# A four-layer graph network on one core: GpSimd's clear behind each gather, 400 bytes in place of 200

## The chip, the cores and the metric

The kernel runs on one core of a Trainium2 chip. The metric is the device time of one execution in microseconds (us), as the median of several executions. The profile is that of one further execution; its times are counted from the start of its span. The engines are TensorE (PE, with its weight loads as PEld), VectorE (DVE), ScalarE (ACT), GpSimd (POOL) and SyncE (SP).

## The reference

The input is x (2708 nodes, 128 features) and a square matrix adj of 2708 x 2708 with some 0.6% of its entries nonzero (and the diagonal). Four layers follow each other, each one as `x = layernorm(x + layer(x, adj))`:

```python
# layer 0: weighted mean
msg = adj.T @ x;  out = msg / adj.sum(axis=0)[:, None]
# layer 1: messages along the edges
messages = gelu((x @ Ws.T)[:, None] + (x @ Wd.T)[None] + b)     # i, j, d
agg = einsum('ijd,ij->id', messages, adj)
out = layernorm(gelu(concat([x, agg]) @ upd_w.T + upd_b) + x) * ln_w + ln_b
# layer 2: h = adj @ (x @ W) + b, batch norm over the nodes, leaky relu
# layer 3: attention, four heads, each
E = leaky_relu((x @ w1)[:, None] + (x @ w2)[None], 0.01)        # i, j, d
s = exp(8 * tanh((E @ a) / 8)) * adj;  s = s / s.sum(-1)
head = leaky_relu(s @ x @ Wlin.T, 0.01);  out = concat(heads) @ w
```

In layers 1 and 3 only the nonzero entries of adj count, so the kernel computes them for the edges alone.

## The kernel before

**Lists.** Layer 0 loads adj by blocks of 128 rows (22 blocks, the last of 20 rows), sums with TensorE, and has VectorE search each row for its nonzero entries. The rows are ranked by their number of entries and their lists scattered to DRAM in that order (lists_dram), in two groups (blocks 0 to 12 and 13 to 21 of the order). Read back, they give a list of neighbours per row (`idx`, `idx3`).

**Layer 1, 22 turns.** A turn handles one block of 128 ranked rows with up to CAPS[b] neighbours each (22 for block 1, 12 for block 11; blocks 0 and 13 have 30 and 29). The turns go in the order TURNS (0 to 18, 21, 19, 20). `messages` takes the neighbours in chunks of up to 8: for each neighbour number k, one gather on GpSimd's queue brings 128 rows of 512 bytes from d_dram, chosen by a column of `idx`, into a slice of a tile `msg` (5 buffers of 8 slices). Then VectorE adds the row's own term to the whole chunk (L907), ScalarE takes the gelu, and VectorE weighs and sums the slices (L895). `update` finishes the block on PE, ACT and DVE and scatters the rows (x_n) to x2_dram from GpSimd's queue (L266). In the first turns the search of the remaining rows and the scatters of their lists run beside this, and the transposing of adj to at_dram; from turn 11 on blocks of layer 2 run (`layer2`, whose gather of at_rows is on GpSimd's queue too). Turn 13 is the first that needs the lists of the second group.

**Layer 2's end.** Batch norm and layer norm over all nodes; t2_dram gets a row per node: 512 transformed features, 128 features, 4 scores (2576 bytes). x3_dram gets the nodes in ranked order by 22 scatters.

**Layer 3, 100 quads.** A quad is four gathers into one tile `g` (9 buffers, GOT), each of 120 to 128 rows of t2_dram chosen by a column of `idx3`. For each quad PE repeats the own terms (z), VectorE adds them (L1566), then multiplies (L1392, L1384), ScalarE sums (L1400), and the softmax and the weighted sum follow two quads at a time. Each of the 24 groups of rows (BLOCKS3) ends in a scatter to the output (out_dram, L266) on GpSimd's queue. PE, DVE and ACT have an order written by hand here (`manual_schedule`); GpSimd's queue does not.

**Order on GpSimd.** The framework's planner orders GpSimd's instructions and assigns buffers, with extra edges where the kernel states them. `gather_spaced` (L258) is used for the gathers of layers 1 and 3: it puts a clear of a small tile `pause` behind each gather and holds the next gather from the same table behind that clear:

```python
    def gather_spaced(dst, table, index):
        before = paused.get(table.name)
        with tc.issue_after(before) if before is not None else nullcontext():
            did = gather(dst, table, index)
        with tc.issue_after(did.ins):
            paused[table.name] = nc.gpsimd.memset(pause, 0).ins
```

Nothing reads `pause`. The gathers of at_rows and all scatters are issued without such a clear.

Of the kernel before, what the change touches and what calls it, by code (L numbers as in the profile page):

```python
# [28 lines left out]
I8 = mybir.dt.int8  # L29
# [56 lines left out]
def gnn_resnorm_kernel(  # L86
# [120 lines left out]
    keep = ctx.enter_context(tc.tile_pool(name="keep", bufs=1))  # L207
# [31 lines left out]
    ones = keep.tile([P, P], FP, name="ones")  # L239
    nc.gpsimd.memset(ones, 1.0)  # L240

    pause = keep.tile([1, 200], I8, name="pause")

    def natural(dram, b0, b1):

# [1862 lines left out]
```

## Time and profile before

| what | value |
|---|---|
| median of 10 runs | 1643.79 us (1632.72 to 1648.18) |
| the profiled execution | 1643.97 us, span 1642.3 us |
| mean granted TensorE clock | 0.709 |
| busy: PE, DVE, ACT, POOL | 1166.6, 1168.7, 772.2, 1094.4 us |
| gathers and clears in layer 1 | 368 each, the gathers starting from 201.0 to 827.7 us |
| gathers and clears in layer 3 | 400 each, the gathers starting from 938.2 to 1577.2 us |

How to read it: a line of costliest groups gives line, engine, operation, output<-input and count, then busy us, mean ns of one, and the idle time of the engine before these instructions with what ended it ("issue": the engine waited for nothing that the profile shows). A line of the timeline gives start, duration, engine, line, operation, and in brackets the idle time before it with its releaser. A gather's span on GpSimd is that of its instruction there, not of the transfer. In the lines of windows, each engine has its busy us and number of instructions.

### The profile page before, as it was taken

What the parts mean: (1) busy time and instruction counts of PE and PEld (TensorE: products, weight loads), DVE (VectorE), ACT (ScalarE), POOL (GpSimd) and SP (SyncE); (2) the same over time, 40 slices, a digit from 0 to 9 for tenths busy, and PEclk for the clock granted to TensorE, in tenths of its full rate; (3) what the DMA queues carried; (4) which work ended last, traced back from release to release, by engine and by line L of the source; (5) the groups of instructions that cost most, each with busy time, mean ns of one, the idle gap of its engine ahead of it and who ended that gap; (6) DMA issues with size and microseconds to landing.
All of it is one profiled execution on the core that took longest, in us unless ns stands there. A gap on an engine that the chain in (4) does not pass through costs nothing. (4 is left out here: it accounts for less than half of the span.)

```text
span 1642.3 us, 24406 instructions
## 1 busy us (share of the span) xinstructions
PE 1166.6 (71%) x5771; PEld 817.5 (50%) x5771; DVE 1168.7 (71%) x4895; ACT 772.2 (47%) x3156; POOL 1094.4 (67%) x1771
## 2 busy tenths in 40 slices
PE   6995523356366664476774787988899988988994
PEld 6984412245245453466663344544455545545553
DVE  8999657387665563556538486888888787788882
ACT  3447566365344321112213455566565566565662
POOL 1002588887787668887722588887887777878730
PEclk9997655555555586687866867677876777777675
DMA  8842476588566724444422677877786765867630
GB/s 260 320 144 94 128 180 178 171 232 243 145 155 177 209 95 114 168 134 170 142 83 76 212 240 198 232 229 206 208 246 187 202 194 164 229 175 228 185 94 8
DMA packets 167682, 289.68 MB, mean 176 GB/s; under 512 B 49600, under 2 KB 121502, under 8 KB 160429
## 3 DMA queue, kind: packets, MB, share of 16 engines
q0 software_dynamic: 60496, 190.77, 40.3%
q1 hardware_dynamic: 99489, 92.57, 18.5%
q10 hardware_dynamic: 7544, 4.69, 1.2%
q8 instruction: 48, 0.79, 0.2%
q14 instruction: 105, 0.86, 0.2%
HBM read 242.51 MB, written 45.36 MB: 175 GB/s over the span
## 5 line engine op out<-in xcount | busy, mean ns | idle before, releaser
L249 POOL DMA_INDIRECT g<-t_dram,idx x400 | 403.7, 1009 | 100.5 <-issue 67.4
L249 POOL DMA_INDIRECT msg<-d_dram,idx x368 | 350.7, 953 | 87.8 <-issue 69.8
L1400 ACT ACTIVATE sum_junk<-g 126x128 bf16<-126x128 f32 (+3 forms) x1024 | 300.7, 295 | 112.9 <-DVE g L1392 76.2
L1369 PE MATMUL z<-x,copies 32*126 32x512 f32 (+3 forms) x800 | 209.0, 880 | 26.4 <-DVE g L1566 25.6
L980 PE MATMUL pt_a<-ident,rows 128*128 128x128 f32 (+2 forms) x475 | 114.0, 394 | 137.4 <-ACT at_sb L985 136.7
L263 POOL MEMSET pause<- 1x200 int8 x768 | 195.5, 255 | 0.1
L1400 ACT ACTIVATION_READ_ACCUMULATOR sum_junk<-g 126x1 f32 (+3 forms) x1024 | 191.5, 187 | 0.0
L1029 PE MATMUL acc<-x_nat,at_rows 128*128 128x128 f32 (+2 forms) x968 | 148.5, 316 | 54.8 <-DMA at_rows<-at_dram,perm 54.5
L1566 DVE TENSOR_TENSOR g<-g,z 126x1536 f32<-126x1536 f32 (+3 forms) x100 | 174.8, 1748 | 12.4 <-PE z L1369 12.4
L1374 PE MATMUL z<-g,ident 126*126 126x512 f32 (+3 forms) x200 | 162.7, 907 | 13.0 <-DMA g<-t_dram,idx 13.0
L1029 PEld LDWEIGHTS acc<-x_nat,at_rows 128*128 128x128 f32 (+2 forms) x968 | 135.4, 223 | 65.3 <-DMA at_rows<-at_dram,perm 52.2
L980 PEld LDWEIGHTS pt_a<-ident,rows 128*128 128x128 f32 (+2 forms) x475 | 82.0, 203 | 162.2 <-ACT at_sb L985 159.4
L1392 DVE SCALAR_TENSOR_TENSOR g<-g,a_ps 126x1536 f32<-126x1536 f32 (+6 forms) x100 | 151.1, 1511 | 0.0
L431 PE MATMUL acc<-x_nat,rows 128*128 128x129 f32 (+3 forms) x1012 | 127.6, 287 | 26.5 <-DMA rows<-in_adj_dram 15.6
L895 DVE SCALAR_TENSOR_TENSOR own<-msg,ls,own 128x128 f32<-128x128 f32 (+1 forms) x302 | 105.6, 350 | 53.6 <-ACT msg L910 49.7
L431 PEld LDWEIGHTS acc<-x_nat,rows 128*128 128x128 f32 (+2 forms) x1012 | 121.9, 196 | 31.8 <-DMA rows<-in_adj_dram 16.7
L1446 PE MATMUL po_s<-wm,g 126*128 126x24 f32 (+6 forms) x800 | 114.9, 296 | 31.3 <-DVE wm L1433 29.6
L1446 PEld LDWEIGHTS po_s<-wm,g 126*128 126x128 f32 (+3 forms) x800 | 111.2, 220 | 46.7 <-DVE wm L1433 40.5
L985 ACT COPY at_sb<-pt_a 128x512 f32<-128x512 f32 (+3 forms) x154 | 68.3, 475 | 85.5 <-DMA at_dram<-at_sb 84.1
L1374 PEld LDWEIGHTS z<-g,ident 126*126 126x126 f32 (+3 forms) x200 | 40.1, 251 | 129.2 <-issue 87.7
L1384 DVE SCALAR_TENSOR_TENSOR g<-z,a 126x128 f32<-126x128 f32 (+3 forms) x400 | 91.9, 285 | 13.4 <-PE z L1374 13.4
L456 DVE FIND_INDEX8 ci<-cv,rows 128x8 uint32<-128x247 f32 (+2 forms) x242 | 98.7, 408 | 0.0
(303 smaller groups left out, 2137.0 us busy)
## 6 DMA issues: line engine op xcount, KB each, us to landing
rows<-in_adj_dram SPq DMA_DIRECT2D x34, 1354.0 KB
at_dram<-at_sb SPq DMA_DIRECT2D x105, 256.0 KB
g<-t_dram,idx POOLq DMA_INDIRECT x400
msg<-d_dram,idx POOLq DMA_INDIRECT x368
t_dram<-t_row SPq DMA_DIRECT2D x21, 256.0 KB
x_s<-dx_dram SPq DMA_DIRECT2D x21, 128.0 KB
at_dram<-at_sb SPq DMA_DIRECT2D x21, 64.0 KB
t_dram<-x_nat SPq DMA_DIRECT2D x5, 256.0 KB
```

What stands on the lines that cost most here:

```text
L249: return nc.gpsimd.indirect_dma_start(out=dst, out_offset=None, in_=table[0:N, :], in_offset=bass.IndirectOffsetOnAxis(ap=index, axis=0),)
L263: paused[table.name] = nc.gpsimd.memset(pause, 0).ins
L431: nc.tensor.matmul(accs0[k][0:m, c0 : c0 + f1 - f0], lhsT=rows[0:n, j0 : j0 + m], rhs=x_nat[0:n, b, f0:f1], start=k not in started, stop=( ...
L895: nc.vector.scalar_tensor_tensor(to, m, v, last, ALU.mult, ALU.add)
L980: nc.tensor.transpose(pt[0:m, j, 0:n], rows[0:n, c0 : c0 + m], ident[0:n, 0:n])
L1029: nc.tensor.matmul(accs2[ib // 4][0:m, (ib % 4) * D : (ib % 4 + 1) * D], lhsT=at[0:n, i0 : i0 + m], rhs=xw[0:n, b, :], start=(k == 0 and i ...
L1369: nc.tensor.matmul(z3[0:e, r, :] if r < 3 else z1[0:e], lhsT=copies[g][rows, j, :], rhs=own[b][1][rows, :], start=True, stop=r < 3, skip_g ...
L1374: nc.tensor.matmul(z1[0:e], lhsT=ident[0:e, 0:e], rhs=g4[0:e, 3, 0:HD], start=False, stop=True, skip_group_check=True,)
L1392: nc.vector.scalar_tensor_tensor(z, z, 0.0, a_ps[0:e].unsqueeze(1).to_broadcast((e, count, HD)), ALU.max, ALU.mult)
L1400: nc.scalar.activation(junk[0:e], g4[0:e, r, hd * D : (hd + 1) * D], AF.Identity, accum_out=sc[0:e, r, hd : hd + 1],)
L1446: nc.tensor.matmul(po[:, p0 * HEADS : (p0 + g) * HEADS], lhsT=g4s[i][0:e, r, HD : HD + D], rhs=wm[0:e, 4 * i + r, :, :], start=True, stop= ...
L1566: nc.vector.tensor_tensor(z, z, z3[0:e], ALU.add)
```

## The change

The tile that is cleared behind each gather has 400 elements of one byte, on one partition, in place of 200. The clears stay as many, at the same places, and still nothing reads them.

```diff
-    pause = keep.tile([1, 200], I8, name="pause")
+    pause = keep.tile([1, 400], I8, name="pause")
```

## The prediction

> **What bounds the kernel now.** I first read the page's costliest groups for the two operations that the change touches, then its slices, then GpSimd's groups with shapes kept apart.
>
> ```profile
> L249 POOL DMA_INDIRECT g<-t_dram,idx x400 | 403.7, 1009 | 100.5 <-issue 67.4
> L249 POOL DMA_INDIRECT msg<-d_dram,idx x368 | 350.7, 953 | 87.8 <-issue 69.8
> L263 POOL MEMSET pause<- 1x200 int8 x768 | 195.5, 255 | 0.1
> ```
>
> There are 768 gathers (400 in layer 3, 368 in layer 1), each followed by a clear of 255 ns, and what idles before the gathers is mostly "issue", which is no waiting for anyone. The timeline of GpSimd shows one such round, and beside it what it looks like without a clear (the scatters of the late rows):
>
> ```profile
> 1200.05 0.95 POOL L249 DMA_INDIRECT g<-t_dram,idx  x1 [0.16 <-issue]
> 1201.00 0.26 POOL L263 MEMSET pause<- 1x200 int8 x1
> 1201.41 0.95 POOL L249 DMA_INDIRECT g<-t_dram,idx  x1 [0.16 <-issue]
> ...
> 297.43 0.96 POOL L266 DMA_INDIRECT dx_dram<-late,rank  x1 [0.30 <-issue]
> 298.69 0.96 POOL L266 DMA_INDIRECT dx_dram<-late,rank  x1 [0.30 <-issue]
> ```
>
> A round is 0.95 + 0.25 + 0.16 = 1.36 us; without a clear 1.26. So 0.16 (gather) and 0.30 (scatter) us of idle time are a floor, and only what is above is a wait. Then I asked for the busy time in windows cut at the stages (columns: PE, PEld, DVE, ACT, POOL, granted clock, DMA share, GB/s):
>
> ```profile
> 201.00:250.00 49.00, 13.68 (x62) 9.40 (x60) 26.97 (x114) 27.92 (x44) 43.27 (x72) 0.58 0.74 190
> 250.00:588.00 338.00, 178.75 (x768) 142.04 (x769) 217.84 (x1105) 155.81 (x321) 255.71 (x404) 0.57 0.68 188
> 588.00:766.00 178.00, 107.00 (x707) 94.84 (x705) 91.75 (x352) 36.86 (x97) 153.06 (x245) 0.73 0.41 128
> 766.00:868.00 102.00, 74.97 (x458) 64.80 (x456) 50.53 (x211) 19.39 (x56) 52.09 (x84) 0.77 0.35 119
> 990.00:1578.00 588.00, 524.98 (x2212) 297.28 (x2206) 478.20 (x1652) 346.93 (x2094) 478.59 (x745) 0.74 0.73 206
> ```
>
> From 201 to 250 and from 588 to 766 POOL is busy for 86 to 88%, and with the floors added it is full: above them it waits 0 and 1.5 us there, by its list of waits. From 250 to 588 it waits 41.8 us above the floors (16.7 of them in one piece, below), from 766 to 830 7.4, and from 990 to 1578 36.6 (19.5 before gathers, 17.1 before scatters of out_dram). In that last window TensorE (89% at a granted clock of 0.74) and VectorE (81%) are the slower side. So one question decides: how far ahead of VectorE's use (the add at L907 in layer 1, at L1566 in layer 3) GpSimd is at each point. Timeline lines, VectorE's under GpSimd's:
>
> ```profile
> 616.54 0.95 POOL L249 DMA_INDIRECT msg<-d_dram,idx  x1 [0.16 <-issue]
> ...
> 619.37 1.09 DVE L907 TENSOR_TENSOR msg<-msg,own 128x896 f32<-128x896 f32 x1 [2.23 <-DMA msg<-d_dram,idx]
> ...
> 764.11 0.95 POOL L249 DMA_INDIRECT msg<-d_dram,idx  x1 [0.16 <-issue]
> ...
> 772.82 1.09 DVE L907 TENSOR_TENSOR msg<-msg,own 128x896 f32<-128x896 f32 x1
> ...
> 1577.15 0.98 POOL L249 DMA_INDIRECT g<-t_dram,idx  x1 [0.19 <-issue]
> ...
> 1599.93 1.75 DVE L1566 TENSOR_TENSOR g<-g,z 120x1536 f32<-120x1536 f32 x1
> ```
>
> The first pair: the add waits for the gather that ended at 617.49, so landing takes 1.9 us behind the gather's end. The other pairs: leads of 7.8 us (last gather of turn 18) and 21.8 us (the last gather). The same pairs elsewhere give 28 to 46 us for the first chunks of turns 2 to 12, and 2.4 to 4.5 us in quads 0 to 8 of layer 3.
>
> **The change part by part.** *The clear.* GpSimd's groups with their shapes give the price of a longer one:
>
> ```profile
> L393 POOL MEMSET caps<- 128x1 f32 x22 | 0.8, 94 | 0.0
> L1298 POOL MEMSET own_x<- 128x768 f32 x1 | 0.7, 742 | 5.9 <-ACT t_row L1238 5.9
> L229 POOL MEMSET lists<- 128x396 f32 x1 | 0.4, 417 | 0.0
> ```
>
> From 1 to 396 elements it is (417 - 94)/395 = 0.82 ns an element, up to 768 (742 - 417)/372 = 0.87; the clear itself, (254 - 94)/199 = 0.80, lies on the same line though its elements are bytes on one partition. So 200 more are 160 to 175 ns; I take 166, from the 396-element row, the nearest in size. A cost below nothing is out: no row falls with size. In all 768 x 0.166 = 127.5 us of GpSimd's time. Nothing else is added: no wait, no transfer, 200 bytes of one partition.
>
> *Who is behind it.* On GpSimd's queue the next gather, and behind that the scatters (L266) and the gathers of at_rows; for those VectorE's adds wait. By stage:
>
> Turn 0 (29 clears before its last gather): 4.8 us, and the adds there wait for the landing. Turns 1 to 12 (191 gathers): 31.7 us, against leads of 28 to 46 us and 25.1 us of waits before 569, so nothing is added; VectorE's idle time there (338 - 218 us) may repay the 4.8. I keep 3.
>
> Turns 13 to 18 (114 gathers, 18.9 us): full, no waits. At the end the lead of 7.8 less a landing of 1.9 leaves 5.9 spare: 13.0 late. Turns 19 to 21 (33 gathers, 5.5 us): the waits of 7.4 us hide them; without that cover 5.5. Layer 1: 3 + 13 = 16, between 13 (turn 0 repaid) and 23 (4.8 + 13 + 5.5).
>
> Layer 3 (399 clears before the last gather, 66.2 us). Cover: the lead at the end, 21.8 - 1.9 = 19.9, and 19.5 of waits before gathers, for buffers that a later gather no longer needs to wait for; 26.8 is left. Of the 17.1 us before scatters, each 1 to 3 us long, most goes too once GpSimd runs later against the adds: I take 15 of 17, since the lost lead is many times a single wait. That leaves 12, between 9.7 and 26.8. Below that, down to nothing, only if VectorE (81% busy) catches up by 0.1 us a quad.
>
> *Shared ports.* Nearly every clear takes 0.25 or 0.26 us, the tile's spread being 254/254/393 ns, so hardly one is held up by another engine. The Trainium skill, SBUF — State Buffer, section Who interferes with whom, says that VectorE in a two-port mode and GpSimd lock each other out for whole instructions; by that a longer clear would be met more often and also hold VectorE longer. Estimate from that page's rule: if each of the 22 writes of x_n met one clear and lost the 0.14 us by which the longest clear exceeds the others, 3 us more; I add nothing for it.
>
> *Sum.* 16 + 12 = 28 us. The profiled execution took 1643.97 us around its span of 1642.3, and the median of the ten is 1643.79, so the two agree: 1644 + 28 = 1672.
>
> **The rivals.** *Nothing gives way.* The waits are dependences that move with the delay, in turns 19 to 21 and before the scatters: 23 + 27 = 50 us, 1694; with 175 ns a clear 1698. For it: the 7.4 us of waits are for x_n, which itself depends on the gathers. Against: the scatter waits in layer 3 come at nine places, the first at 1146, when by the sum GpSimd would already be some 23 us later (140 clears at 0.166) against waits of 3 us at most.
>
> *The order (not slower).* GpSimd's queue is ordered by the framework's planner in all layers; if a longer clear changes its plan, scatters can come to stand elsewhere. The place:
>
> ```profile
> 568.69 0.94 POOL L249 DMA_INDIRECT at_rows<-at_dram,perm  x1 [0.30 <-issue]
> 586.65 1.00 POOL L266 DMA_INDIRECT x_dram<-x_n,perm  x1 [17.02 <-DVE x_n L332]
> 587.95 0.97 POOL L249 DMA_INDIRECT msg<-d_dram,idx  x1 [0.30 <-issue]
> ```
>
> Turn 13's gathers stand behind a scatter that waits 16.7 us above its floor, while their indices lay ready at 500. Another order would give that, and with the 6.0 us before x_n in turns 18 to 21 and the 6.5 before the scatters of the lists up to 29 us back: 1643. It decides from about 23 us on. Against: the opposite, a worse order, is as open, and nothing says that the planner sees this wait.
>
> *The clear grows by less than its bytes.* At half, 80 ns: turn 0 2.3, turns 13 to 18 9.1 - 5.9 = 3.2, layer 3 31.9 - 39.4, nothing: at most 1649. Against it speak the three rows.
>
> **How the numbers follow.** The forecast 0.68 (1655 to 1690: 9.7 or nothing in layer 3, 13 to 23 in layer 1, up to full layer 3), nothing gives way 0.15, the order 0.13, less growth 0.04. The range 1652 to 1698 leaves out most of the order's and the small growth's cases and a little above, about 0.19. A measurement of this kernel tells about 0.3% (5 us) from no change. Slower by more: 0.68 + 0.15 and a little of the last two, 0.86; the same: half of the last two, 0.09; faster: a part of the order's, 0.05.
>
> **What would show it.** The clear's row at 414 to 429 ns; rounds of 1.53 us; the lead at the last gather below 8 us instead of 21.8; waits before out_dram near 2 us; POOL's waits from 250 to 569 near nothing; the first gather of layer 3 (938.2) some 16 us later and its length 12 us more. If the first gather of layer 3 comes earlier than now, the order decided; if the lead at the end is still over 15, VectorE and TensorE slowed down or caught up otherwise, and my cover is wrong.

## The result and the profile after

The changed kernel takes 1707.9 us (median of 9 runs, 1705.28 to 1718.9), the kernel before, beside it, 1643.89 (31 runs): a ratio of 1.0397, 95% interval 1.0376 to 1.0419. That is 64 us more, where 28 were forecast and 54 was the end of the range. Wherever the text says "after" without more, it means the profiled execution of that comparison (span 1704.8 us); "before" is the one of the prediction (1642.3).

On three of the four chips on which the experiments ran, the kernel before took 1848 to 1896 us and not 1644 to 1648, and there the longer clear makes it faster; each experiment is therefore read against the kernels that ran beside it on the same chip, or against kernels with the same length of clear.

The costliest groups of after, to be set against the three lines shown first in the prediction:

```profile
L249 POOL DMA_INDIRECT g<-t_dram,idx x400 | 403.3, 1008 | 81.8 <-issue 58.5
L249 POOL DMA_INDIRECT msg<-d_dram,idx x368 | 351.0, 954 | 71.0 <-issue 61.7
L263 POOL MEMSET pause<- 1x400 int8 x768 | 323.8, 422 | 0.1
```

The clear takes 422 ns in place of 255, 128 us in all; the gathers cost what they did, and wait 35 us less. Of the 128 us, 64 reach the end. Where they pass is seen by the same pairs as before, GpSimd's last gather and VectorE's add:

```profile
795.26 0.97 POOL L249 DMA_INDIRECT msg<-d_dram,idx  x1 [0.16 <-issue]
...
801.37 1.09 DVE L907 TENSOR_TENSOR msg<-msg,own 128x896 f32<-128x896 f32 x1
...
1657.69 0.98 POOL L249 DMA_INDIRECT g<-t_dram,idx  x1 [0.19 <-issue]
...
1664.23 1.75 DVE L1566 TENSOR_TENSOR g<-g,z 120x1536 f32<-120x1536 f32 x1
```

Turn 18's last add comes at 801.4 (before 772.8), with a lead of 5.1 us (7.8); the last add of layer 3 at 1664.2 (1599.9), with a lead of 5.6 (21.8). By stages, from the timelines of VectorE's adds and GpSimd's gathers:

| point | before | after | later by |
|---|---|---|---|
| turn 0, last add | 249.1 | 257.9 | 8.8 |
| turn 12, last add | 597.7 | 607.9 | 10.2 |
| turn 18, last add | 772.8 | 801.4 | 28.6 |
| turn 21, last add | 842.8 | 875.3 | 32.5 |
| layer 3, first gather | 938.2 | 972.0 | 33.8 |
| layer 3, last gather | 1577.2 | 1657.7 | 80.5 |
| layer 3, last add | 1599.9 | 1664.2 | 64.3 |

So 34 us arise ahead of layer 3 and 30 in it. The waits that were to give way in layer 3 did not: above a floor of 0.30 us the 20 scatters to the output that stand between gathers wait 17.0 us in all, and before it was 17.1. They don't wait for their rows. VectorE writes the rows of four groups together (y_s, L1518). The first four in before, with two of their scatters, and then the same in after:

```profile
1134.22 1.11 DVE L1518 TENSOR_SCALAR y_s<-y_s,sums,var 128x128 f32<-128x128 f32 x4
...
1142.45 1.02 POOL L266 DMA_INDIRECT out_dram<-y_s,to  x1 [0.18 <-issue]
1146.48 1.00 POOL L266 DMA_INDIRECT out_dram<-y_s,to  x1 [3.01 <-PE z L1369]
```

```profile
1178.92 1.30 DVE L1518 TENSOR_SCALAR y_s<-y_s,sums,var 128x128 f32<-128x128 f32 x4
...
1199.55 1.02 POOL L266 DMA_INDIRECT out_dram<-y_s,to  x1 [0.17 <-issue]
1203.44 1.00 POOL L266 DMA_INDIRECT out_dram<-y_s,to  x1 [2.87 <-PE z L1374]
```

The rows of the scatter that waits here were written 12 us before its start in before, 24 us in after. At all the places with a wait it is 6 to 18 us in before and 21 to 33 in after, so GpSimd does run later against the rows, and the waits stay. What they wait for is the scatter ahead. By the semaphore records of the traces, the scatter of 1142.45 has landed at 1145.63, 0.85 us before the next one starts, and that of 1199.55 at 1202.60, 0.84 before. The same holds at all 19 places (9 in before, 10 in after) where such a scatter waits more than 0.1 us above the floor: it starts 0.77 to 0.88 us behind the landing of the scatter ahead of it. The instructions named in the brackets ended at that time, but did not write these rows.

The queue itself does not ask for such a wait. The kernel declares the scatters to dx_dram independent of each other (`declare_no_dep`, L757), and those that stand in a row start 1.26 to 1.32 us apart, each before the one ahead has landed (291 to 300 us in before). For the scatters to the output (L1522) it declares nothing.

### The profile page after: what moved, and what is told of

It reads as the page before. It is cut to its first block, busy times and chain, and to the rows that moved or that the text cites. A ratio compares the mean times of both kernels' runs of the same rounds, so it can differ in the third digit from the quotient of the medians.

```text
span 1704.8 us, 24421 instructions
## 1 busy us (share of the span) xinstructions
PE 1174.0 (69%) x5771; PEld 825.8 (48%) x5771; DVE 1173.6 (69%) x4895; ACT 772.6 (45%) x3156; POOL 1222.1 (72%) x1771
## 5 line engine op out<-in xcount | busy, mean ns | idle before, releaser
L263 POOL MEMSET pause<- 1x400 int8 x768 | 323.8, 422 | 0.1
L1369 PE MATMUL z<-x,copies 32*126 32x512 f32 (+3 forms) x800 | 204.8, 885 | 24.2 <-DVE g L1566 22.9
L1029 PE MATMUL acc<-x_nat,at_rows 128*128 128x128 f32 (+2 forms) x968 | 144.7, 309 | 100.1 <-DMA at_rows<-at_dram,perm 99.7
L1374 PE MATMUL z<-g,ident 126*126 126x512 f32 (+3 forms) x200 | 167.7, 933 | 39.0 <-DMA g<-t_dram,idx 38.8
L1029 PEld LDWEIGHTS acc<-x_nat,at_rows 128*128 128x128 f32 (+2 forms) x968 | 130.9, 216 | 110.9 <-DMA at_rows<-at_dram,perm 95.3
L431 PEld LDWEIGHTS acc<-x_nat,rows 128*128 128x128 f32 (+2 forms) x1012 | 125.1, 200 | 30.1 <-DMA rows<-in_adj_dram 14.6
L1384 DVE SCALAR_TENSOR_TENSOR g<-z,a 126x128 f32<-126x128 f32 (+3 forms) x400 | 91.9, 286 | 21.8 <-PE z L1374 21.7
L910 ACT ACTIVATE msg<-msg 128x896 f32<-128x896 f32 (+4 forms) x55 | 50.4, 916 | 114.0 <-DVE msg L907 91.2
## 6 DMA issues: line engine op xcount, KB each, us to landing
at_dram<-at_sb SPq DMA_DIRECT2D x105, 256.0 KB
t_dram<-t_row SPq DMA_DIRECT2D x21, 256.0 KB
t_dram<-x_nat SPq DMA_DIRECT2D x5, 256.0 KB
```

The costliest lines, as they stand in the source:

```text
L431: nc.tensor.matmul(accs0[k][0:m, c0 : c0 + f1 - f0], lhsT=rows[0:n, j0 : j0 + m], rhs=x_nat[0:n, b, f0:f1], start=k not in started, stop=( ...
L1029: nc.tensor.matmul(accs2[ib // 4][0:m, (ib % 4) * D : (ib % 4 + 1) * D], lhsT=at[0:n, i0 : i0 + m], rhs=xw[0:n, b, :], start=(k == 0 and i ...
L1369: nc.tensor.matmul(z3[0:e, r, :] if r < 3 else z1[0:e], lhsT=copies[g][rows, j, :], rhs=own[b][1][rows, :], start=True, stop=r < 3, skip_g ...
L1374: nc.tensor.matmul(z1[0:e], lhsT=ident[0:e, 0:e], rhs=g4[0:e, 3, 0:HD], start=False, stop=True, skip_group_check=True,)
```

## A path that the prediction did not follow

The forecast let turns 1 to 12 hide their clears, because the gathers there lead VectorE's adds by 28 to 46 us. The lead is real, but VectorE also stands still three times there for something else that GpSimd issues. The first place, in the kernel before (timeline; SPq are DMAs issued by SyncE):

```profile
299.95 0.96 POOL L266 DMA_INDIRECT dx_dram<-late,rank  x1 [0.30 <-issue]
...
302.40 0.92 SPq L1005 DMA_DIRECT2D column_sum<-dx_dram  x2
303.41 1.80 SPq L987 DMA_DIRECT2D at_dram<-at_sb  x4
...
307.13 0.59 ACT L985 COPY at_sb<-pt_a 128x512 f32<-128x512 f32 x1 [25.90 <-DMA at_dram<-at_sb]
...
310.19 0.36 DVE L895 SCALAR_TENSOR_TENSOR own<-msg,ls,own 128x128 f32<-128x128 f32 x1 [27.84 <-ACT msg L910]
```

Read it downwards: the last scatter of the late rows leaves GpSimd's queue at 301, behind 65 gathers with their clears. A small load of SyncE (column_sum) waits for it, and the transfers of at_sb stand behind that load in the same queue. ScalarE waits 25.9 us for a free at_sb, with the gelu of turn 1's last chunk behind it, and VectorE 27.8 us for that gelu. The other two places are the same with the scatters of the lists. In after:

```profile
464.31 1.00 POOL L266 DMA_INDIRECT lists_dram<-lists,rank  x1 [0.30 <-issue]
466.72 1.71 SPq L608 DMA_DIRECT2D lists<-lists_dram  x4
...
470.37 0.15 DVE L644 CAST to<-node 128x1 int32<-128x1 f32 x1 [15.16 <-DMA node<-lists_dram]
...
511.33 0.91 POOL L266 DMA_INDIRECT lists_dram<-lists,rank  x1 [0.30 <-issue]
513.37 0.36 SPq L590 DMA_DIRECT2D ls<-lists_dram  x1
...
516.94 0.51 DVE L596 CAST idx<-ls 128x256 int32<-128x256 f32 x1 [17.31 <-DMA ls<-lists_dram]
```

Before, these two stops end at 456.4 and 499.5, behind scatters that start at 447.65 and 494.44, with 149 and 179 clears ahead of them in GpSimd's queue. They now end 14 and 17 us later. The 177 clears that are ahead of the last scatter in after take 30 us more, by 0.167 each; GpSimd's own waits ahead of it fell from 22 to 9 us, which covers the other 13. VectorE goes on where GpSimd has put the scatter; how far the gathers lead plays no part.

From 517 to turn 12's end 7 of the 17 us are made up. Nothing shows that this is the clear's doing. Before has a fourth stop in this stretch, 8.7 us at 578.3 for a load of `node` (L644), which after lacks. The same program on another chip (after_again, below) has it, 9.1 us at 595.4, and its turn 12 ends at 613.6 instead of 607.9.

## The experiments

**Price or order.** A longer clear also changes the planner's plan: in after the order of the instructions differs on all five engines. To part the two, the planner is shown clears of one length, and once it is done each clear's output is set to another. The orders then are exactly those of the kernel before (price_only) or after (order_only).

```diff
+def resize(nc):
+    for function in nc.m.functions:
+        for block in function.blocks:
+            for i, one in enumerate(block.instructions):
+                if one.name in CLEARS:
+                    at = one.outs[0]
+                    at = copy.replace(at, ap=[list(at.ap[0]), [1, CLEARS[one.name]]], bass_ap=None)
+                    block.instructions[i] = copy.replace(one, outs=[at])
...
-            paused[table.name] = nc.gpsimd.memset(pause, 0).ins
+            clear = nc.gpsimd.memset(pause[:, 0:200], 0).ins
+            CLEARS[clear.name] = 400
+            paused[table.name] = clear
...
         gnn_resnorm_kernel(tc, *args)
+    resize(nc)
```

price_only (planned with 200, 400 run):

> The planner is shown clears of 200 bytes, so that every engine's order is that of the kernel before; the clears that run have 400 bytes. Price theory (the added 0.167 us of each clear is nearly all of the loss; few waits give way): the time of the changed kernel, 1700 to 1710 us, with layer 3's first gather some 34 us later than before (938 us). Order theory (the planner, seeing longer clears, re-ordered layers 0 to 2, and that costs as much as the price there): 1685 to 1692, first gather of layer 3 some 16 us later, as the prediction's sum for layer 1 had it. The prediction's own sum in whole: 1672.

order_only (planned with 400, 200 run):

> The reverse: the planner is shown clears of 400 bytes, so that every engine's order is that of the changed kernel; the clears that run have 200 bytes. Price theory: 1644 within 5 us. Order theory: 1655 to 1665, all of the difference before layer 3's first gather.

price_layer1 and price_layer3 (order of before, 400 in one layer alone):

> The order of the kernel before; 400 bytes run in layer 1's 368 clears alone, 200 in layer 3's. Price theory: 1644 + 34 = 1678, all of it before layer 3's first gather. Order theory: 1644 + 16 = 1660.

> The order of the kernel before; 400 bytes run in layer 3's 400 clears alone, 200 in layer 1's. If the waits before the scatters of out_dram stay (66.6 us of clears, less 19.5 of waits before gathers, less some 18 of lead): 1644 + 29 = 1673. If they give way as the prediction had it: 1644 + 12 = 1656. The order of layer 3 is the planner's for GpSimd alone, so both theories on order give the same here.

All four ran on one chip, on which the kernel before took 1885 us: price_only 1731.0 (ratio 0.917, 0.9128 to 0.9213), order_only 1903.36 (1.0096, 1.0066 to 1.0126), price_layer1 1787.7 (0.9472, 0.9403 to 0.9541), price_layer3 1827.53 (0.9699, 0.9656 to 0.9742). The sign is the opposite of the result's, and the two layers' gains (97 and 58 us) add to the whole 154. Hence the two again on the same chip, with the changed kernel itself and a shorter clear beside them.

> Clears of 400 bytes in the order of the kernel before, a second time, since on the chip of the first time the kernel before itself took 1885 us against 1644. If the kernel before takes about 1644 here: price theory 1700 to 1710, order theory 1685 to 1692. If it takes about 1885: 1731, as the first time, for the pace theory: on such a chip gathers closer than about 1.5 us make TensorE and those who wait for it stand still for 5 to 16 us at a time, and a longer clear takes that away.

> Clears of 200 bytes in the order of the changed kernel, a second time. Kernel before at 1644: price theory 1644 within 5 us, order theory 1655 to 1665. Kernel before at 1885: 1903 again.

> The changed kernel on the same chip as the other two, so that price and order can be summed against it. Kernel before at 1644: 1708. Kernel before at 1885: 1710 to 1750, faster than the kernel before, by the pace theory.

> 100 bytes run in each clear, in the order of the kernel before; a round is 1.28 us in place of 1.36. Kernel before at 1644: price theory alone, faster by what saturated stretches give back: about 13 us in layer 1 and little in layer 3, where TensorE and VectorE set the pace, 1625 to 1635. Pace theory with its threshold just below 1.36 us there: the stalls of the other chip set in, 1680 or more. Kernel before at 1885: pace theory 1900 or more.

Beside a kernel before of 1886.58 us: price_only_2 1729.89, order_only_2 1909.53 (ratio 1.0112, 1.0072 to 1.0151), after_again 1724.31 (0.9137, 0.9101 to 0.9172), clear_100 1948.54 (1.0324, 1.025 to 1.0399). The other order is worth 6 us at clears of 400 (1729.9 to 1724.3) and costs 18 to 23 at 200: on this chip the order is not what moves the time. The clear's length does it, here in the other direction.

**What is different there.** The kernel before, profiled once under these conditions (before_again), and a clear of 300 in the order of before.

> The kernel before itself, for its profile under the conditions of these runs. In the profile shown with it (1643.97 us) no wait without a visible releaser was longer than 4 us. If the conditions of the chip make such waits (theory: what lasts 200 us longer here is engines standing still behind TensorE while the gathers come every 1.36 us), VectorE and ScalarE show at least 20 waits of over 4 us put down to 'issue' or 'remote', 100 us or more in all, and the clear stays at 255 ns. Rival, the chip is just slower: every row's mean ns grows, by 15% for a time of 1885, and no new waits show.

> The kernel before in its own order (planned with clears of 200), while clears of 300 run (a round of 1.44 us). Where the kernel before takes about 1885 us and the one with clears of 400 in the same order 1730: a graded effect gives 1790 to 1825; a threshold between 200 and 400 gives a time close to one end (under 1760 or over 1860). Where the kernel before takes about 1644: half of the clears' 128 us, less the cover of layer 1's waits and layer 3's lead, gives 1650 to 1670.

Measured: 1890.81 us for before_again, and 1782.2 for clear_300 (ratio to a kernel before of 1896.21: 0.9419, 0.9363 to 0.9475), a graded effect and no threshold, though 8 us below the range I gave for it. The page of before_again says that no engine but TensorE has become slower:

```profile
span 1889.1 us, 24406 instructions
...
PE 1245.3 (66%) x5771; PEld 868.9 (46%) x5771; DVE 1174.7 (62%) x4895; ACT 775.6 (41%) x3156; POOL 1096.2 (58%) x1771
```

VectorE, ScalarE and GpSimd are busy as long as before (1168.7, 772.2, 1094.4). What is new are stops. One in layer 3 and one in layer 1, from the timeline:

```profile
1117.72 0.31 ACT L1400 ACTIVATE sum_junk<-g 128x128 bf16<-128x128 f32 x1 [1.74 <-remote]
1119.86 0.31 ACT L1400 ACTIVATE sum_junk<-g 128x128 bf16<-128x128 f32 x1 [1.74 <-remote]
...
1122.02 1.75 DVE L1566 TENSOR_TENSOR g<-g,z 128x1536 f32<-128x1536 f32 x1 [8.42 <-remote]
1123.83 2.08 PE L1369 MATMUL z<-x,copies 32*128 32x512 f32 x6 [11.43 <-issue]
```

```profile
677.51 0.29 PEld L1029 LDWEIGHTS acc<-x_nat,at_rows 128*128 128x128 f32 x1 [0.43 <-issue]
678.23 0.29 PEld L1029 LDWEIGHTS acc<-x_nat,at_rows 128*128 128x128 f32 x1 [0.43 <-issue]
...
679.82 0.40 ACT L1018 ACTIVATE weighed<-ones,column_sum 128x128 f32<-128x128 f32 x1 [16.02 <-remote]
```

ScalarE's sums start 2.14 us apart, though VectorE's products, their input, ended at 1113.6. TensorE's weight loads of one train start 0.72 us apart; from 679.64 on, 24 loads of the same train take 4.10 us. VectorE waits for both: 8.4 us in the first stop, and 13.4 in the second, for a gelu behind ScalarE's wait. GpSimd's gathers run on throughout the first stop, and in the second until 677. I added up VectorE's waits of over 4 us that are put down to "issue" or "remote", from 200 us on:

| clear | kernels | such waits of VectorE | us |
|---|---|---|---|
| 100 | clear_100 | 30 | 226 |
| 200 | before_again, order_only, order_only_2 | 21, 24, 26 | 155, 188, 219 |
| 300 | clear_300 | 11 | 75 |
| 400 | price_only, price_only_2, price_only_3, after_again | 4, 1, 1, 1 | 56, 5, 5, 5 |
| 200, first comparison | before | 0 | 0 |

So where these stops occur, they follow the pace of the gathers, and a longer clear takes away more of them than it costs. With 400 in layer 1 alone one stop (34 us) is left ahead of layer 3 and 11 (67 us) stay in it; with 400 in layer 3 alone 10 (73 us) stay ahead of it and one (5 us) is left in it. GpSimd stops as well, before gathers: 11 such waits in before_again (82 us), 19 in clear_100 (134 us), none in the kernels with 400 throughout. Whether these follow from the other engines' stops, the profile doesn't say.

**Mean pace or single pause.** Clears of 4 and 400 in turn, in the order of before:

```diff
-            CLEARS[clear.name] = 400
+            n = len(CLEARS)
+            CLEARS[clear.name] = 400 if n % 2 else 4
```

> The kernel before in its own order; the clears behind the gathers have 4 and 400 elements in turn, so two gathers take (0.95 + 0.09 + 0.16) + (0.95 + 0.42 + 0.16) = 2.73 us, as with clears of 200 (2 x 1.36 = 2.72). Theory 'pace' (what stops the other engines is the mean pace of the gathers): the time is that of the kernel before in the same call, within 15 us. Theory 'single pause' (each pause of over 0.25 us lets something pass that the gathers hold up): it differs by over 15 us, faster by up to 150 if a pause behind every second gather is enough. Where the kernel before takes about 1644, both give the same within 5 us.

1828.85 us, ratio 0.9911 (0.9875 to 0.9947) to a kernel before of 1847.64. That is 19 us less, beyond my limit of 15 for "pace". But beside it clears of 400 throughout give 118 us (price_only_3, 1730.14), so a pause of 0.42 us behind every second gather alone brings only a sixth of that: most of it goes by the mean pace.

**Layer 3's scatters.** The output scatters that stand between gathers are collected and issued behind the last gather; the order of all other engines stays.

```diff
-                scatter(out, to3[0:n, b : b + 1], y[0:n, b, :])
+                if fetched[0] is None:
+                    waiting.append((b, n))
+                else:
+                    scatter(out, to3[0:n, b : b + 1], y[0:n, b, :])
...
+        fetched[0] = paused[t2_dram.name]
+        with tc.issue_after(fetched[0]):
+            for b, n in waiting:
+                scatter(out, to3[0:n, b : b + 1], y[0:n, b, :])
         while closing or finishing:
             step()
```

> The changed kernel (clears of 400), with the 20 output scatters of layer 3 that stood between gathers moved behind the last gather; the orders of TensorE, VectorE, ScalarE and SyncE are those of the changed kernel. Theory A (the mis-sized term: the scatters' waits of some 17 us don't give way to a later GpSimd, and the gathers set layer 3's pace): the last gather comes by 17 + 20 x 1.26 = 42 us earlier at most, and the time falls by 20 to 42 us against the changed kernel. Theory B (VectorE and TensorE set the pace in layer 3, the scatters' waits cost nothing): the time falls by less than 8 us, and the lead of the gathers over VectorE's adds grows instead.

> The kernel before (clears of 200), with the same 20 scatters moved behind the last gather and nothing else. Where VectorE and TensorE set layer 3's pace (lead of 21.8 us at the last gather before), nothing is won: within 8 us of the kernel before. If the pace of the gathers itself does harm here (a round of 1.36 us is too fast, as clears of 100 and 400 suggest), the gathers come closer together and the time is longer by 5 us or more. If the gathers bound even here, it is faster by 10 us or more.

scatters_last_400 takes 1717.98 us (ratio 0.907, 0.903 to 0.911) against 1724.31 of the changed kernel on another chip: by the time alone theory B's case. But the gathers of layer 3 take 646.6 us from the first to the last in place of 684.2 (after_again), as theory A has it, and their lead grows too. From the first add to the last it is 663.4 in place of 683.8, so the waits and the scatters themselves make 20 us of layer 3 here. Only 6 us reach the end, because 24 scatters in a row wait for each other; such a row in both_400 (below):

```profile
1645.08 0.94 POOL L266 DMA_INDIRECT out_dram<-y_s,to  x1 [1.60 <-DMA out_dram<-y_s,to]
1647.61 0.97 POOL L266 DMA_INDIRECT out_dram<-y_s,to  x1 [1.59 <-DMA out_dram<-y_s,to]
1650.13 0.96 POOL L266 DMA_INDIRECT out_dram<-y_s,to  x1 [1.55 <-DMA out_dram<-y_s,to]
```

2.5 us each and not 1.26, behind each other's landing, which here the profile itself names: the last one starts 42 us after the last add in scatters_last_400, 31 in after_again. scatters_last_200 takes 1887.58 (ratio 0.9959, 0.9931 to 0.9986): with clears of 200 the scatters' place is worth some 8 us (3 to 13).

**Turns 0 to 12 and 13 to 21.** The base is price_only again; then 560 elements in place of 400 in one part of layer 1. In these three kernels the stops are nearly absent (1, 0 and 0 waits of VectorE).

```diff
-    pause = keep.tile([1, 400], I8, name="pause")
+    pause = keep.tile([1, 560], I8, name="pause")
...
-            CLEARS[clear.name] = 400
+            n = len(CLEARS)
+            CLEARS[clear.name] = 560 if 221 <= n < 368 else 400
```

(t0_560 has `n < 221`.)

> The kernel before in its own order, with clears of 400 running: the base for the two kernels below. Where the kernel before takes about 1885 it was 1730; where it takes about 1644 the gathers' price alone should give 1700 to 1712, if the planner's other order is worth nothing.

> As the base, but the 147 clears of turns 13 to 21 have 560 elements: 160 x 0.83 ns = 0.133 us more each, 19.5 us in all. If the gathers set the pace of these turns (POOL full, no slack in the leads): turn 21 ends 16 to 20 us later behind turn 13's first add, and the time is 14 to 20 us longer. If the forecast's account holds (a third is hidden by leads and waits): 10 to 13 us. If something else sets the pace: under 5.

> As the base, but the 221 clears of turns 0 to 12 have 560 elements: 0.133 us more each, 29.4 us in all, 4 of them in turn 0. If leads of 28 us and more hide turns 1 to 12, as forecast: the time is 0 to 6 us longer. If they come through: 15 to 29 us.

price_only_3 1730.14, t13_560 1751.4, t0_560 1744.48. Turns 13 to 21 pass the clear on in full: 21.3 us for 147 clears of 0.133 us more (19.5); from turn 13's first add to turn 21's last it is 274.6 us against 256.0. Of turns 0 to 12's 29.4 us, 14.3 come through, between my two cases. By the trace the last scatter of the lists starts 15.7 us later (535.50 against 519.78), and turn 12's last add 15.7 (638.9 against 623.2).

**SyncE's queue.** The changed kernel with the second group's column sums loaded behind turn 11's own rows; GpSimd's order stays.

```diff
             if i == 10:
-                column_sums_of(1)
+                with tc.issue_after(loaded[0].ins):
+                    column_sums_of(1)
```

(`loaded[0]` is the last load of own rows.) The planner answers this by moving instructions of other engines too: VectorE's order differs from after's at 106 places, TensorE's at 34, ScalarE's at 18. both_400 has this and the scatters' move.

> The changed kernel (clears of 400) with one thing moved: the two loads of the second group's column sums come behind the load of turn 11's own rows on SyncE's queue, in place of some 140 places earlier; GpSimd's order is the same. Theory 'SyncE's queue': ScalarE's wait of 27 us for at_dram (at 351 us) goes, the gelu of turn 2's last chunk no longer waits for it, turn 12's last add comes 10 us earlier or more, and the time falls from 1724 to between 1700 and 1715. Rival 'no path there' (the wait just moves to the next load or scatter): turn 12's last add within 4 us of 613, time 1720 to 1728.

> The changed kernel with both moves: the column sums' loads later and layer 3's 20 scatters behind the last gather. If the two places are independent, the gains add: the scatters' 6 us (1724 to 1718) plus the column sums' gain, so 1694 to 1709 by the theory 'SyncE's queue', and 1714 to 1722 by the rival.

Here the kernel before took 1647.76 us, and the profiles of the two kernels show no stop of VectorE, ScalarE, TensorE or GpSimd. columns_later_400: 1717.67, ratio 1.0419 (1.0402 to 1.0436), against 1.0397 for the changed kernel: nothing gained, as the rival had it (turn 12's last add at 612.1, within 4 us of its 613; the time 2 us below its range). The stop at 351 is gone, and turn 3's first add comes at 338.3 in place of 365.5. But the next stop takes it back; columns_later_400's timeline:

```profile
459.56 1.00 POOL L266 DMA_INDIRECT lists_dram<-lists,rank  x1 [0.30 <-issue]
...
465.42 0.15 DVE L644 CAST to<-node 128x1 int32<-128x1 f32 x1 [29.43 <-DMA node<-lists_dram]
```

VectorE now waits 29.4 us here, where it was 15.2, for a scatter that GpSimd reaches only 5 us earlier. both_400: 1703.84, ratio 1.0336 (1.0319 to 1.0354). Between these two kernels, whose orders differ on GpSimd alone, the scatters' move is worth 13.8 us: layer 3's gathers take 643.7 us from the first to the last in place of 685.1, and the adds 660.6 in place of 683.9. So with clears of 400 the gathers set layer 3's pace on a chip without the stops too. Neither kernel beats the kernel before where that takes 1648 us; where it takes 1896, scatters_last_400 beats it by 9%.

## Why the prediction was wrong

The sum came to 28 us and 64 were measured, 36 more. Rounded, layer 3 has 18 of these, turns 13 to 21 have 9, turns 0 to 12 have 7, and 1 arises between turn 21 and layer 3.

**Right:** the price of the clear (166 ns; 167), and with it the rival "less growth" is out; the rounds (1.53 us); the lead at the last gather (under 8; 5.6); GpSimd's waits from 250 to 569 near nothing (4.6 us in after's stretch from 258 to 588); and the waits before layer 3's gathers, which gave the 19.5 us that the sum took (the gathers' stretch grew by 46.7 us for 66.6 of clears). Nothing had to be added for shared ports: the clears take 421/421/557 ns (minimum, median, maximum), and VectorE is busy for 1173.6 us in place of 1168.7.

**Layer 3, 12 us: the step that failed most.** It gave 30. The wrong term is "15 of 17" for the waits before the scatters, of which 0.1 us went (17.1 to 17.0). The sum let them go "once GpSimd runs later against the adds", so it took them for waits for the rows. GpSimd did run later, but a scatter waits for the landing of the scatter ahead of it, which comes later by as much. The lead gave 16 us and not 20. 66.6 - 19.9 (waits before gathers) - 16.2 (lead) = 30.5; the stretch of the adds grew by 30.1.

**Turn 0, 4.8 us of which 3 stay.** 8.8 in after, 3.0 of them before the first gather (204.0 against 201.0). That start varies from 200.3 to 204.0 among the 20 profiles, with clears of 200 as of 400 (203.9 in order_only, 200.6 in price_only), so the 3.0 need not be the clear's. In columns_later_400, which starts at 201.0, it is 4.7. The size was right, the repayment was not.

**Turns 1 to 12, nothing: the path left out.** I asked only how far the gathers lead the adds of their own messages. The scatters of the late rows and of the lists stand on the same queue, and VectorE stands 52 us behind them in before (27.8, 16.0 and 8.5). t0_560 shows half of a longer clear passing there, columns_later_400 that a stop removed ahead of a later one is given back at that one. In after the stage ends 10.2 us late instead of 3; at the last of the three stops it was 17.

**Turns 13 to 18, 13.0 us; 19 to 21, nothing.** Measured 18.4 and 3.9, of 18.9 and 5.5. The lead of 5.9 us that I spent was spent by 2.7 (7.8 to 5.1), and the waits for x_n moved with the delay, as the rival "nothing gives way" said: in before and in after these scatters start 0.28 us behind the end of VectorE's write of their rows. t13_560 confirms it: all of the clear comes through. Layer 1 so gives 34 us, not 16.

**The rivals.** "Nothing gives way" (50 us) named both places and was 14 short: in turns 0 to 12 (10.2 against 4.8), in turns 13 to 18 (18.4 against 13.0) and by the lead that layer 3 kept (3.7). For x_n its reason was right; for the scatters to the output it was right by luck, since their rows lay ready. My argument against it, that GpSimd would be 23 us late against waits of 3 us, took a wait that begins anew behind each scatter for one that ends at a fixed time. "The order" was real, in that the planner changed all queues, but the runs with the orders exchanged give it 6 us of gain at 400, not 29. The wait of 17 us before turn 13 is 3.2 in after, but 15.5 in after_again, the same program; it goes with VectorE's fourth stop, and turn 13's gathers started 5.5 us later all the same, not earlier.

What stays open: how much of after's first 10 us belongs to the other order, since price_only never ran where the kernel before takes 1644; and what the output scatters cost once they are declared independent, which no run here did.

## What to carry to other kernels

A lead of one stream over its consumer covers a delay for that stream alone. Before taking a cover, list every other instruction on the same queue and who waits for each, also by way of another engine's queue. Before counting a wait as cover, find what ends it: compare its end with the write of the data and with the landing of the transfer ahead, since the releaser that a profile names can be chance. A wait for data that the delayed work itself feeds moves with it (x_n), and so does a wait for the transfer ahead on the same queue (the output scatters); neither is a cover. A stop removed ahead of a later one that doesn't depend on it is given back there. And when an experiment's base time differs from the one to be explained, the base is profiled first: the same change can have the other sign.

## What the runs showed of the hardware

The same program, with the same busy time on VectorE, ScalarE and GpSimd, took 1644 and 1648 us in two of the comparisons and 1848 to 1896 on three chips, by stops of over 4 us of TensorE, ScalarE, VectorE and, before its gathers, GpSimd. They grow more frequent the faster GpSimd issues gathers (a gather each 1.36 us in layer 3, with clears of 100: 226 us of VectorE's waits in all; each 1.61, with clears of 400: 5 to 56). Of 49 such waits of VectorE, ScalarE and TensorE in before_again, 39 end in windows of 4 us with a granted clock of 0.50 (227 of all 422 windows have it). But 0.50 is granted in about half of before's windows too (166 of 360), without such stops, so it is not shown to be the cause.

The Trainium skill, Runtime: NRT & Kernel Launch, section Instruction fetch mechanics, says that an engine's instructions come in blocks of 256 by a queue of its own, mostly hidden. The traces have the packets of the instruction queues, and they don't look like the cause: those of 8 KB and more are 158 in before and 159 in before_again, with a median of 0.44 us in both and at most 2.4 and 1.6 us. None starts in either of the two stops shown (none between 1101.7 and 1125.5 us, none between 658.3 and 711.4). What holds these engines back was not found.

The scatters to the output, which the kernel doesn't declare independent, wait for each other's landing: 2.5 us each in a row; spread between gathers each costs 1.3 us of GpSimd's time and 0.85 of waits on average (17.0 us over 20 in after). The scatters to dx_dram, which it does declare independent, start 1.26 to 1.32 us apart in a row.
